# A fused attention and local-attention transformer kernel: K's projection around P's transposes, second parts of a norm's steps inside K's rotation, and the order of the first slots

## The chip, the cores and the metric

The kernel runs on one core of one Trainium2 chip. Its time is the device time of one execution in microseconds (us). A core has TensorE (PE, with its weight loads shown apart as PEld), VectorE (DVE), ScalarE (ACT), GpSimd (POOL) and SyncE (SP), which issues most DMAs. Each engine works through its own queue in order and waits for the others by semaphores.

## The reference

The input x has 4 batches of 512 tokens of width 128. First comes a pre-norm full attention with 16 heads of 64:

```python
x = x + attn(layernorm(x), Wq, Wk, Wv, Wr)
x = x + ffn_stack(layernorm(x), Wqkv, q_scale, k_scale, Wo, ln_g, ln_b, W1, b1, W2, b2)
```

The second line holds six layers, each of them

```python
x = attn_layer(shift_tokens(x), ...) + x
x = ffn_layer(shift_tokens(x), ...) + x
```

where shift_tokens moves half of the features by one token. attn_layer projects to q, k and v (3 x 1024 features), normalises each head of q and k by its length, scales and rotates them by position, and attends within windows of 32 tokens and the window before. ffn_layer is a layer norm with gain and bias, a projection to 2 x 341 features, a product of one half with the GELU of the other, and a projection back to 128. Everything is in 32-bit floats.

## The kernel before

The first attention takes the first 568 us of the trace and isn't touched. The layers work on *units* of 128 tokens: 6 layers x 4 batches x 4 tiles = 96 units, in the order layer, batch, tile. `slot(n, ...)` writes the instructions of one step of a software pipeline, by hand, and every engine then runs its own part in this order. In slot n four units are at work: `u` = unit n has its scores, exponentials and P times V; `prev` = n-1 its output projection and residual; `nxt` = n+1 its transposes of Q and K; `new` = n+2 its projections and rotations. The order in a slot is, by engine:

- TensorE: scores of u (L652, L663), Q's projection of new (L517), norm matmuls if any (L97, L106 or L114), output projection of prev (L720), the two groups of P's transposes (L625), K's projection, first half of P times V (L695), Q's transposes of nxt, V's projection, second half of P times V, K's transposes, an FFN chunk or the FFN's output if any (L763, L764, L783), and the transposes of the attention's output o.
- VectorE: maximum and subtraction for u (L673, L675), norm steps, the residual of prev (L728), Q's rotation (L538, L542), sum of Q's squares (L533), division of the first half of the attention's output (L704, L705), K's rotation, division of the second half, sum of K's squares, the start of the inverse norms (L557, L81, L82), and the FFN's gate (L771) or its residual (L786).
- POOL: for a first tile the shifted copies (L150 to L152) and, for a new layer, the rotation tables (L164, which waits for a small DMA); the rest of a norm's rsqrt (L84 to L87, 12 small operations), the two sums that end the rotations of Q and K (L553), the copy of K's last window (L644), 12 operations of the inverse norms, and the two multiplications by them (L561).
- ACT: the exponential (L681), the squares of Q and K (L528), all copies out of PSUM (L607, L628), GELU (L767), the square in a norm's mean step (L101).
- SP: the DMAs that lay out V in windows (L615 to L619), and the weights of the next layer behind the last unit of a layer.

PSUM holds three pairs of banks, called two0 to two2, which turn by one with each slot, and two single banks (`one_t`, in turn) for all transposes, the output projection and the norm's matmuls. So P's second group of transposes takes the bank that the output projection of the same slot was in, and waits for the residual to read it.

The FFN of a batch works beside the slots that follow its last unit. With n a multiple of 4, `plan` sets the shift at slot n, the three steps of its norm (mean, var, scale) at slots n+1, n+2 and n+3, between Q's projection and the output projection, the three chunks at n+3, n+4 and n+5 and the output at n+6, ahead of o's transposes. So a slot whose number leaves 1, 2 or 3 when divided by 4 has a norm step, and the others have the shifts. The first FFN chunk comes in slot 7. The norm of the last batch of the first attention, called `late`, runs ahead of slots 1, 2 and 3.

A layer norm's steps are: mean (a matmul with 1/128, the difference on VectorE, L99, and its square on ACT), var (small matmuls, L106, then the start of an rsqrt on VectorE, L81 and L82, and the rest on POOL), scale (transposes that spread the factor, L114, then the product, L118, and the gain and bias, L120).

Of the kernel before, what the change touches and what calls it, by code (L numbers as in the profile page):

```python
# [8 lines left out]
F32 = mybir.dt.float32  # L9
# [6 lines left out]
P = 128  # L16
# [16 lines left out]
def body(ctx: ExitStack, tc: tile.TileContext, a, out: bass.AP):  # L33
# [52 lines left out]
            eng.tensor_scalar(t, t, -0.5, 1.5, ALU.mult, ALU.add)  # L86
            eng.tensor_tensor(y if k < 2 else v, y, t, ALU.mult)  # L87

    def layernorm_steps(state, bank, inT, outT, g=None, b=None, eng=nc.vector, nt=NT, temp=tmpt):

        w = nt * P

        def mean():
            m = bank()[:, 0:w]
            mm(m, lhsT=avg, rhs=inT(), start=True, stop=True)  # L97
            xc = state["xc"] = temp()[:, 0:w]
            nc.vector.tensor_tensor(xc, inT(), m, ALU.subtract)  # L99
            sq = state["sq"] = temp()[:, 0:w]  # L100
            nc.scalar.activation(sq, xc, AF.Square)  # L101

        def var():
            v = bank()
            for t in range(nt):
                mm(v[:, t : t + 1], lhsT=state["sq"][:, t * P : (t + 1) * P], rhs=avg[:, 0:1], start=True, stop=True)  # L106
            rs = state["rs"] = small.tile([P, NT], F32, tag="rs", name="rs")[:, 0:nt]
            nc.vector.tensor_scalar(rs, v[:, 0:nt], EPS, None, ALU.add)  # L108
            rsqrt(rs, nt, eng)

        def scale():
            bc = bank()[:, 0:w]
            for t in range(nt):
                nc.tensor.transpose(  # L114
                    bc[:, t * P : (t + 1) * P], state["rs"][:, t : t + 1].to_broadcast([P, P]), ident
                )
            h = state["h"] = outT()
            nc.vector.tensor_tensor(h, state["xc"], bc, ALU.mult)  # L118
            if g is not None:
                nc.vector.tensor_scalar(h, h, g, b, ALU.mult, ALU.add)  # L120

        return mean, var, scale

# [48 lines left out]
    with tc.manual_schedule():  # L172
# [105 lines left out]
        class Rows:  # L278


            def __init__(self, b, c, t):
                self.b, self.c, self.t = b, c, t
# [212 lines left out]
    def two_t(k, name):  # L495
        k = (part[0] + k) % 3
        return ps.tile([P, 2, 512], F32, tag=f"two{k}", name=name, bufs=1)
# [7 lines left out]
    def flat(pt):  # L505
        return pt.rearrange("p a n -> p (a n)")
# [4 lines left out]
            self.i, self.b, self.T = i, b, T  # L511
            self.r = [None, None]

    def project(u, j):
        p = two_t((1, 2, 1)[j], "ps_proj")
        for c in range(2):
            mm(  # L517
                p[:, c, :],
                lhsT=u.xs[:, u.T * P : (u.T + 1) * P],
                rhs=wpart[j][:, c * 512 : (c + 1) * 512],  # L520
                start=True,
                stop=True,
            )
        return flat(p)

    def square(u, j):
        u.sq = s2a.tile([P, INNER], F32, tag="t1", name="sq", bufs=3)
# [4 lines left out]
            u.ss = small.tile([P, 2 * HEADS], F32, tag="ss", name="ss")  # L532
        nc.vector.tensor_reduce(u.ss[:, j * HEADS : (j + 1) * HEADS], heads(u.sq), AX.X, ALU.add)  # L533

    def rotate(u, j):
        t0 = u.r[j] = s2a.tile([P, INNER], F32, tag="rot", name="rot", bufs=6)
        lt, pf, half = u.lt, u.p[j], HD // 2
        nc.vector.tensor_tensor(  # L538
            heads(t0), heads(pf), lt[:, u.T, 2 * j].unsqueeze(1).to_broadcast([P, HEADS, HD]), ALU.mult
        )  # L540
        t1 = u.t1 = s2a.tile([P, INNER], F32, tag="t1", name="t1", bufs=3)
        nc.vector.tensor_tensor(  # L542
            t1.rearrange("p (h t d) -> p h t d", t=2, d=half),
            pf.rearrange("p (h t d) -> p h t d", t=2, d=half)[:, :, ::-1, :],
            lt[:, u.T, 2 * j + 1]
            .rearrange("p (t d) -> p t d", t=2)
            .unsqueeze(1)
            .to_broadcast([P, HEADS, 2, half]),
            ALU.mult,
        )  # L550
# [129 lines left out]
        u.prf = u.pr.rearrange("p c a n -> p (c a n)")  # L680
        nc.scalar.activation(u.prf, u.prf, AF.Exp)  # L681

    def transpose_p(u):
        u.pT = s2.tile([P, NC, P], F32, tag="pT", name="pT", bufs=2)
        for g in range(2):
            transposed(u.prf, g, u.pT, 0)

    def times_v(u, g, k=0):
        if g == 0:
# [41 lines left out]


    class Ffn:
        def __init__(self, u, t0=0, nt=NT, temp=tmpt, pair=None, eng=None):
            self.i, self.b, self.u, self.t0, self.nt, self.us, self.st = u.i, u.b, u, t0, nt, [], {}
            self.temp, self.pair = temp, pair or (lambda f: (tmpt(), tmpt()))
            self.mean, self.var, self.scale = layernorm_steps(
                self.st,
                one_t,
                lambda: self.xs,  # L740
                lambda: s2.tile([P, S], F32, tag="hT", name="hT", bufs=2)[:, 0 : nt * P],
                vecs[:, u.i, 0:1],
                vecs[:, u.i, 1:2],
                eng or nc.vector,
                nt,
                temp,
            )

        def shift(self):
# [81 lines left out]
        for v in units[u.n : u.n + NT]:  # L831
            v.xs, v.lt, v.p = xs, lt, [None] * 3

    def do_project(u, j):
        u.p[j] = project(u, j)
        if u.b + 1 == B and u.T + 1 == NT and u.i + 1 < L:
            wpart[j] = load_part(u.i + 1, j)

    def first_slot():
# [23 lines left out]
    def slot(n, norm, move, geglu):  # L863

        u, prev, nxt, new = unit(n), unit(n - 1), unit(n + 1), unit(n + 2)
        part[0] = n % 3
        begin(unit(n + 4))  # L870
        if u:
            scores(u)
            exponents(u)
        if new:
            do_project(new, 0)
            square(new, 0)
        if n == -1:
            y = one_t()
            project_out1(B - 1, y)
        for f in norm:  # L880
            f()
        if prev:
            project_out_2(prev)
            if prev.b + 1 == B and prev.T + 1 == NT and prev.i + 1 < L:
                wo_w[0] = load_wo(prev.i + 1)
            residual(prev)
        for f in move:
            f()
        if u:
            transpose_p(u)  # L890
        if new:
            rotate(new, 0)
            add_rotated(new, 0)
            sum_squares(new, 0)
        if n == -1:
            residual1(B - 1, y)
        if new:
            do_project(new, 1)
            square(new, 1)
        if u:  # L900
            times_v(u, 0)
        if nxt:
            transpose_q(nxt)
        if new:
            do_project(new, 2)
            v_windows(new, follower(new))
            rotate(new, 1)
            add_rotated(new, 1)
        if u:
            times_v(u, 1)  # L910
        if new:
            sum_squares(new, 1)
        if nxt:
            transpose_k(nxt)
        if n == -1:
            third_step()
        if nxt:
            carry_k(nxt, follower(nxt))
        if new:
            inverse_norms(new)  # L920
            over_norm(new, 0)
            over_norm(new, 1)
        for f in geglu:
            f()
        if u:
            transpose_o(u)

    with tc.manual_schedule():
        begin(units[0])
        late = norm_x1(one_t, B - 1)  # L930


        norm, move, geglu = {}, {}, {}

        def plan(steps, n, *fs):
            steps.setdefault(n, []).extend(fs)
# [3 lines left out]

        end = len(units)
        for n in range(NT, end - NT, NT):
            f = Ffn(units[n - 1], eng=nc.gpsimd)
            plan(move, n, f.shift)
            for k, g in enumerate((f.mean, f.var, f.scale)):
                plan(norm, n + 1 + k, g)
            for k in range(3):
                plan(geglu, n + 3 + k, at(f.chunk, k, 2))
            plan(geglu, n + 6, at(f.out, 2, n + 6 == end - 2))
        third, seq = f, Ffn(units[end - NT - 1], eng=nc.gpsimd)  # L950
        plan(move, end - 4, seq.shift)
        plan(norm, end - 3, seq.mean)
# [24 lines left out]
        def tail():  # L977

            exponents(u)
            seq.scale()  # L980
            project_out_2(prev)
            residual(prev)
            most.shift()
            transpose_p(u)
            most.mean()
            part[0] = 1
            times_v(u, 0, 0)
            times_v(u, 1, 1)
            part[0] = 0
            gate = seq.chunk(0, 0, True)  # L990
            transpose_o(u)
            gate()
            most.var()
            project_out_2(u)
            residual(u)
            last.shift()
            seq.chunk(1, 1)
            last.mean()
            most.scale()
            last.var()  # L1000
            seq.chunk(2, 2)
            for k in range(2):
                most.chunk(k, k)
            last.scale()
            most.chunk(2, 2)
            seq.out(0, True)
            for k in range(3):
                last.chunk(k, (k + 1) % 3)
            seq.finish()
            most.out(1, True)  # L1010
            last.out(2, True)
            most.finish()
            last.finish()

        first_slot()
        for n in range(-1, end - 1):
            if 1 <= n < 4:
                late[n - 1]()
            slot(n, norm.get(n, ()), move.get(n, ()), geglu.get(n, ()))
        tail()  # L1020

# [92 lines left out]
```

## Time and profile before

| | |
|---|---|
| median of 3 runs | 2260.88 us (2259.3 to 2263.07) |
| the profiled execution | 2261.35 us |
| its span on the core | 2259.6 us |
| first scores of slot 0 | 568.5 us |
| slots 37, 38, 39, 40, from scores to scores | 17.13, 18.37, 17.03, 16.54 us |
| slots 0 to 7 | 18.06, 16.89, 16.39, 15.14, 16.85, 15.96, 17.57, 17.30 us |
| granted clock of TensorE, mean | 0.993 |

A row of the timeline has the start and the length in us, the engine, the line of the code, the operation and its tiles, and in brackets the idle time just before it with what ended it. A row of the view of waits has the engine and line that waited, what it waited for, and the total in us, the number of waits and the longest one. A row of the view of windows has, for one stretch, its length, the busy time of PE, PEld, DVE, ACT and POOL (with the number of instructions), the granted clock of TensorE, the share of the DMA engines' time and GB/s.

### The profile page before, as it was taken

The page shows a single profiled execution, that of the slowest core. Times are in us where ns is not written, and L with a number is a line of the kernel's source. Part 1 is how long each engine was busy: PE and PEld are TensorE (multiplying, and loading weights), DVE is VectorE, ACT ScalarE, POOL GpSimd, SP SyncE. Part 2 cuts the span into 40 slices and gives each one's busy share as a digit, 9 for nine tenths or more (in the row PEclk, how much of TensorE's full clock was granted, in tenths as well). Part 3 has the DMA queues.
Part 4 walks back from the last instruction along what each step waited for, and adds up shares of the span by engine and source line. Part 5 has one row for each costly group of instructions (what it writes and reads, how often), then busy time and mean ns, then how long its engine had stood idle before and what let it go on. Part 6 is the DMA issues. An engine that isn't in the chain of part 4 may idle for free.

```text
span 2259.6 us, 82472 instructions
## 1 busy us (share of the span) xinstructions
PE 2183.4 (97%) x35150; PEld 1435.4 (64%) x35150; DVE 1710.3 (76%) x2501; ACT 1365.9 (60%) x2589; POOL 1511.7 (67%) x2281
## 2 busy tenths in 40 slices
PE   7999999999899999999999999999999999999997
PEld 5565655554666666666666666666666666666665
DVE  4676667676778888878788788878888788888874
ACT  4665656564556656666566656666566666666663
POOL 2554545465787777777777777777777777777762
PEclk8999999999999999999999999999999999999999
DMA  3000000000322233232322323223232223322221
GB/s 117 1 1 1 1 1 1 1 1 9 75 69 60 69 87 73 57 76 69 85 69 62 78 66 86 66 67 73 71 85 63 66 71 87 76 63 70 60 67 28
DMA packets 91064, 125.77 MB, mean 56 GB/s; under 512 B 25422, under 2 KB 39500, under 8 KB 90700
## 3 DMA queue, kind: packets, MB, share of 16 engines
q1 hardware_dynamic: 89996, 118.79, 21.4%
q8 instruction: 280, 4.59, 0.9%
q10 hardware_dynamic: 704, 1.70, 0.2%
q14 instruction: 84, 0.69, 0.1%
HBM read 20.31 MB, written 1.05 MB: 9 GB/s over the span
## 4 chain that ended last, share of the span: by engine, by line
PE 58%; DVE 12%; POOL 3%; issue 2%; ACT 1%; POOLq 0%; ACTq 0%
PE ps_proj L517 18%; PE ps_one L625 14%; PE ps_att L663 6%; PE ps_att L695 6%; PE ps_one L720 3%; PE ps_proj L783 3%; PE ps_proj L763 3%; PE ps_proj L764 3%; DVE y L82 2%; DVE mx L673 2%; DVE pr L675 2%; PE ps_att L652 1%; DVE hT L120 1%; POOL rot L553 1%; DVE t L542 1%
## 5 line engine op out<-in xcount | busy, mean ns | idle before, releaser
L553 POOL TENSOR_TENSOR rot<-rot,t 128x1024 f32<-128x1024 f32 x192 | 453.9, 2365 | 255.8 <-DVE t L542 188.5
L517 PE MATMUL ps_proj<-wqkv,xs 128*128 128x512 f32 x1152 | 557.0, 606 | 5.9 <-DVE tmp_t L771 5.0
L344 POOL TENSOR_TENSOR pr<-pr,den 128x1024 f32<-128x1024 f32 x128 | 241.0, 1894 | 247.5 <-DVE den L341 239.6
L561 POOL TENSOR_TENSOR rot<-rot,ss 128x1024 f32<-128x1024 f32 x192 | 361.5, 1904 | 7.4
L517 PEld LDWEIGHTS ps_proj<-wqkv,xs 128*128 128x128 f32 x1152 | 197.5, 191 | 157.2 <-issue 143.2
L528 ACT ACTIVATE sq<-ps_proj 128x1024 f32<-128x1024 f32 x192 | 195.3, 1017 | 127.5 <-PE ps_proj L517 126.8
L681 ACT ACTIVATE pr<-pr 128x1024 f32<-128x1024 f32 x96 | 101.5, 1058 | 260.8 <-DVE pr L675 260.8
L542 DVE TENSOR_TENSOR t<-ps_proj,lt 128x1024 f32<-128x1024 f32 x192 | 233.2, 1215 | 19.6 <-POOL rot L553 19.2
L538 DVE TENSOR_TENSOR rot<-ps_proj,lt 128x1024 f32<-128x1024 f32 x192 | 233.0, 1214 | 19.5 <-ACT sq L528 19.4
L533 DVE TENSOR_REDUCE ss<-sq 128x16 f32<-128x1024 f32 x192 | 231.6, 1206 | 0.0
L330 ACT ACTIVATE pr<-ps_sc,nm 128x128 f32<-128x128 f32 (+3 forms) x448 | 220.6, 511 | 5.7 <-DVE nm L317 5.2
L317 DVE TENSOR_REDUCE nm<-ps_sc 128x2 f32<-128x1024 f32 x128 | 155.9, 1218 | 82.8 <-PE ps_sc L305 82.7
L673 DVE TENSOR_REDUCE mx<-ps_att 128x16 f32<-128x1024 f32 x96 | 117.5, 1224 | 127.1 <-PE ps_att L663 127.1
L625 PE MATMUL ps_one<-ident,rot 128*128 128x128 f32 x1536 | 209.6, 279 | 0.9 <-POOL rot L561 0.9
L720 PEld LDWEIGHTS ps_one<-aT,wo 128*128 128x128 f32 x1536 | 183.0, 192 | 24.6 <-issue 23.9
L720 PE MATMUL ps_one<-aT,wo 128*128 128x128 f32 x1536 | 189.1, 276 | 0.4 <-DVE rs L108 0.3
L625 PEld LDWEIGHTS ps_one<-ident,rot 128*128 128x128 f32 x1536 | 164.7, 141 | 19.8 <-POOL rot L561 1.1
L695 PEld LDWEIGHTS ps_att<-vw,pT 64*32 64x32 f32 x9216 | 101.1, 105 | 108.3 <-issue 108.0
L607 ACT COPY vt<-ps_proj 128x512 f32<-128x512 f32 x192 | 103.2, 590 | 101.3 <-PE ps_proj L517 101.3
L355 PEld LDWEIGHTS ps_pt<-ident,pr 128*128 128x128 f32 x1024 | 118.2, 142 | 56.9 <-issue 47.1
L84 POOL TENSOR_TENSOR yt<-y 128x32 f32<-128x32 f32 (+2 forms) x384 | 88.0, 229 | 93.6 <-DVE y L82 47.5
L355 PE MATMUL ps_pt<-ident,pr 128*128 128x128 f32 x1024 | 135.7, 275 | 3.0 <-POOL pr L344 2.7
(173 smaller groups left out, 4083.0 us busy)
## 6 DMA issues: line engine op xcount, KB each, us to landing
vw<-vt SPq DMA_DIRECT2D x1152, 65.0 KB, 2.0
vw_first<-vt SPq DMA_DIRECT2D x336, 65.0 KB, 2.0
wqkv<-in_wqkv_dram SPq DMA_DIRECT2D x18, 512.0 KB, 9.2
wo<-in_wo_dram SPq DMA_DIRECT2D x6, 512.0 KB
w<-in_w_dram SPq DMA_DIRECT2D x6, 341.0 KB, 3.5
xr<-in_x_dram SPq DMA_DIRECT2D x3, 256.0 KB
scales<-in_scales_dram SPq DMA_DIRECT2D x6, 128.0 KB, 3.2
w<-in_w_dram SPq DMA_DIRECT2D x12, 64.0 KB, 2.9
```

The source lines that it names most:

```text
L330: nc.scalar.activation(self.pr[:, h, cols], self.sc[:, h, cols], AF.Exp, bias=self.nm[:, part_, h : h + 1], accum_out=self.den[:, part_, h ...
L344: nc.gpsimd.tensor_tensor(self.pr, self.pr, self.den[:, 0].unsqueeze(2).to_broadcast([P, 2, S]), ALU.mult)
L355: nc.tensor.transpose(pt[:, k * P : (k + 1) * P], self.pr[:, h, k * P : (k + 1) * P], ident)
L517: mm(p[:, c, :], lhsT=u.xs[:, u.T * P : (u.T + 1) * P], rhs=wpart[j][:, c * 512 : (c + 1) * 512], start=True, stop=True,)
L533: nc.vector.tensor_reduce(u.ss[:, j * HEADS : (j + 1) * HEADS], heads(u.sq), AX.X, ALU.add)
L538: nc.vector.tensor_tensor(heads(t0), heads(pf), lt[:, u.T, 2 * j].unsqueeze(1).to_broadcast([P, HEADS, HD]), ALU.mult)
L542: nc.vector.tensor_tensor(t1.rearrange("p (h t d) -> p h t d", t=2, d=half), pf.rearrange("p (h t d) -> p h t d", t=2, d=half)[:, :, ::-1, :],
L553: nc.gpsimd.tensor_tensor(u.r[j], u.r[j], u.t1, ALU.add)
L561: nc.gpsimd.tensor_tensor(heads(u.r[j]), heads(u.r[j]), u.ss[:, j * HEADS : (j + 1) * HEADS].unsqueeze(2).to_broadcast([P, HEADS, HD]), AL ...
L625: nc.tensor.transpose(tp[:, c * P : (c + 1) * P], src[:, (4 * g + c) * P : (4 * g + c + 1) * P], ident)
L695: mm(o[j * W : (j + 1) * W, h, c * (HD + 1) : (c + 1) * (HD + 1)], lhsT=u.pT[h * HD : (h + 1) * HD, 4 * g + c, j * W : (j + 1) * W], rhs=u ...
L720: mm(y[:, 0:P], lhsT=wo_w[0][:, c, :], rhs=u.aT[:, c, :], start=(c == 0), stop=(c == NC - 1))
```

## The change

It has five parts.

1. K's projection is made in two halves of 512 columns. In a slot with a norm step the first half stands between the two groups of P's transposes, in another slot ahead of both; the second half follows the second group. Slot 0 has the whole projection ahead of P's transposes, and Q's transposes of nxt ahead of the first half of P times V.
2. The norm steps of the FFNs in the loop put their second part on a list, `later`: the square in mean, the rsqrt in var, gain and bias in scale. K's rotation runs that list between its two operations on VectorE.
3. In slots without an FFN part (up to slot 6) K's rotation and its sum on POOL come behind the second half of P times V instead of ahead of it.
4. The three steps of `late` run as norm steps of slots 0, 1 and 2.
5. In the last layer the transposes and the output DMA that finish a batch (`finish`) come one slot after the FFN's output (slot 91 instead of 90).

```diff
+        def then(f):
+            f() if later is None else later.append(f)
...
-            nc.scalar.activation(sq, xc, AF.Square)
+            then(lambda: nc.scalar.activation(sq, xc, AF.Square))
...
-            rsqrt(rs, nt, eng)
+            then(lambda: rsqrt(rs, nt, eng))
...
-                nc.vector.tensor_scalar(h, h, g, b, ALU.mult, ALU.add)
+                then(lambda: nc.vector.tensor_scalar(h, h, g, b, ALU.mult, ALU.add))
...
-    def project(u, j):
-        p = two_t((1, 2, 1)[j], "ps_proj")
-        for c in range(2):
+    def project(u, j, c0=0, c1=2):
+        p = u.p[j] if c0 else two_t((1, 2, 1)[j], "ps_proj")
+        u.p[j] = p
+        for c in range(c0, c1):
...
-    def rotate(u, j):
+    def rotate(u, j, between=()):
...
+        for f in between:
+            f()
...
-    def transpose_p(u):
-        u.pT = s2.tile([P, NC, P], F32, tag="pT", name="pT", bufs=2)
-        for g in range(2):
-            transposed(u.prf, g, u.pT, 0)
+    def transpose_p(u, g):
+        if g == 0:
+            u.pT = s2.tile([P, NC, P], F32, tag="pT", name="pT", bufs=2)
+        transposed(u.prf, g, u.pT, 0)
...
+        if n == 0:
+            do_project(new, 1)
         if u:
-            transpose_p(u)
+            if norm:
+                transpose_p(u, 0)
+        if new and n != 0:
+            do_project(new, 1, 0, 1)
+        if u:
+            if not norm:
+                transpose_p(u, 0)
+            transpose_p(u, 1)
         if new:
             rotate(new, 0)
             add_rotated(new, 0)
...
         if new:
-            do_project(new, 1)
+            if n != 0:
+                do_project(new, 1, 1)
             square(new, 1)
+        if nxt and n == 0:
+            transpose_q(nxt)
         if u:
             times_v(u, 0)
-        if nxt:
+        if nxt and n != 0:
             transpose_q(nxt)
         if new:
             do_project(new, 2)
             v_windows(new, follower(new))
-            rotate(new, 1)
-            add_rotated(new, 1)
+            if geglu:
+                rotate(new, 1, later)
+                add_rotated(new, 1)
         if u:
             times_v(u, 1)
         if new:
+            if not geglu:
+                rotate(new, 1, later)
+                add_rotated(new, 1)
+            later.clear()
             sum_squares(new, 1)
...
-        norm, move, geglu = {}, {}, {}
+        norm, move, geglu = {k: [f] for k, f in enumerate(late)}, {}, {}
...
-            f = Ffn(units[n - 1], eng=nc.gpsimd)
+            f = Ffn(units[n - 1], eng=nc.gpsimd, later=later)
...
-            plan(geglu, n + 6, at(f.out, 2, n + 6 == end - 2))
+            ends = f.i + 1 == L
+            plan(geglu, n + 6, at(f.out, 2, ends))
+            if ends and n + 6 < end - 2:
+                plan(geglu, n + 7, f.finish)
...
-            if 1 <= n < 4:
-                late[n - 1]()
             slot(n, norm.get(n, ()), move.get(n, ()), geglu.get(n, ()))
```

## The prediction

> **What bounds the kernel now.** First the page's busy times and chain, for which engine sets the end.
>
> ```profile
> span 2259.6 us, 82472 instructions
> PE 2183.4 (97%) x35150; PEld 1435.4 (64%) x35150; DVE 1710.3 (76%) x2501; ACT 1365.9 (60%) x2589; POOL 1511.7 (67%) x2281
> PE 58%; DVE 12%; POOL 3%; issue 2%; ACT 1%; POOLq 0%; ACTq 0%
> ```
>
> TensorE does. DVE's 12% of the chain is the time in which TensorE hangs on VectorE, and the view of waits says where in the layers:
>
> ```profile
> PEld ps_one L625 <- DVE xT L728: 32.6, 69, 1.7
> PEld ps_one L625 <- ACT pr L681: 8.5, 27, 3.0
> ```
>
> L625 is the helper for all transposes; the form that waits is P's. Its second group takes the PSUM bank that the output projection's y was in, so it waits until the residual (L728) has read y. The first group waits for the exponential (L681). Next the timeline of a settled stretch, slots 38 and 39 (18.37 and 17.03 us, start of scores to start of scores; 37 and 40 take 17.13 and 16.54), VectorE and POOL around L728:
>
> ```profile
> 1227.64 3.76 POOL L561 TENSOR_TENSOR rot<-rot,ss 128x1024 f32<-128x1024 f32 x2
> 1229.60 1.83 DVE L82 TENSOR_SCALAR y<-yt 128x4 int32<-128x4 int32 x1
> 1231.34 0.28 DVE L728 TENSOR_TENSOR xT<-ps_one,xT 128x128 f32<-128x128 f32 x1
> 1241.12 0.18 DVE L82 TENSOR_SCALAR y<-yt 128x32 int32<-128x32 int32 x1
> ...
> 1245.26 3.77 POOL L561 TENSOR_TENSOR rot<-rot,ss 128x1024 f32<-128x1024 f32 x2
> 1248.09 1.22 DVE L120 TENSOR_SCALAR hT<-hT,vecs 128x512 f32<-128x512 f32 x1
> 1249.56 0.66 PE L625 MATMUL ps_one<-ident,pr 128*128 128x128 f32 x4 [0.25 <-DVE xT L728]
> ```
>
> L82 needs 0.18 us, but takes 1.83 and ends when POOL's pair of multiplications ends (1231.43 against 1231.40); L120 ends 0.28 after its pair (1249.31 against 1249.03), so 0.28 is its own price. Both stand ahead of L728. POOL's long operations hold VectorE's SBUF-to-SBUF tensor_scalar back, and through L728 they hold TensorE.
>
> **The change, part by part.** n mod 4 tells the slots apart: 1 has the FFN norm's mean, 2 its var, 3 its scale, 0 the shifts on POOL.
>
> (1) K's projection is split around P's second group: 0.9 us (2 of the L517 pieces of 1.88 per four) lie between the groups in slots with a norm, ahead of both in the others. It needs nothing late: its PSUM pair was read in the slot before. No instruction is added, and the split is free: in the starts of single matmuls the one after a change between a 128x512 and a transpose follows at the usual 0.43 or 0.11 us. L728 finishes about 0.35 us after the output projection and the second group now comes 1.35 after it. So the 32.6 us go, but for some 2 in the last two slots, which are not changed, and 1.5 in slots 1 to 7, counted below: -29. In the 22 slots with n mod 4 = 0 the wait for the exponential, 0.18 each on the weight load, is covered too: -4.
>
> (2) The second parts of the norm's steps go between K's two rotation operations. L81, L82 and L120 then run while POOL has finished the first rotation's sum (L553, 2.36 us) and waits for K's: 0.2 + 0.2, and 0.28. Here a rule is weighed. The Trainium skill, "SBUF — State Buffer", Who interferes with whom, says that a tensor_scalar in a two-port mode and a GpSimd instruction exclude each other for a whole instruction, whoever is first. The rows agree, and the rule also speaks against the change: it moves POOL's sums as well. In a var slot POOL's 12 small steps (3.3 us, 1231.5 to 1234.8) leave the place ahead of Q's sum for that ahead of K's, so K's sum starts about 2.5 us after its operands; L557, L81 or L82 then collide with it. By the free rows they cost 0.6, by the rule up to 2.4 more. I take the rule: L786, next on VectorE and the reader of the FFN's PSUM pair, then ends at 1243.9 on the trace's clock, and Q's next projection, which takes that pair, is due at 1243.9 with slot 38's gain taken off. The cover is used up: 0.05 x 22 = +1 (0 to 0.45 each). ACT's square of the mean slot (0.62) falls between V's copies and K's; Q's next projection has 0.5 us left: nothing.
>
> (3) What is late next. VectorE's string from L728 to the end of L82 was 9.7 us in slot 39 and gets L120's 0.28 and a longer block at L557 (about +0.3), while TensorE gains 1.1 in slots 38 and 39. POOL's multiplications then end 7.9 us into slot 40, not 7.1; the two shifts (2.85) follow, Q's sum starts at 10.75, not 9.96, K's second rotation waits for it, and the gate (L771), which frees Q's PSUM pair, ends 18.2 us after the slot's start. Q's projection could begin at 18.0. I take 0.3 x 17 = +5 (0 to 0.8 each). In the other five (12, 28, 44, 60, 76) POOL has a layer's table to make as well, and the stall there already exists:
>
> ```profile
> 1345.79 2.28 DVE L81 TENSOR_SCALAR yt<-ss 128x32 int32<-128x32 int32 x1
> 1349.11 3.68 PE L517 MATMUL ps_proj<-wqkv,xs 128*128 128x512 f32 x4 [1.75 <-DVE tmp_t L771]
> 1349.00:1352.00 3.00, 2.89 (x4) 1.34 (x5) 2.41 (x3) 0.52 (x1) 2.19 (x10) 0.54 0.38 85
> ```
>
> POOL is 0.8 us later there: 5 x 0.8 = +4. The third line is a window's row; its clock, 0.54, is why the projection takes 3.68 and not 1.88. The skill's "TensorE: Matmul & The Clock Gate" (HAM clock gate) puts the half rate after an idle window of about 3.4 us; here a wait of 1.75 was enough, though 2.16 in slot 0 was not. By the page new stalls under 2 us cost only themselves, by this row perhaps 1.7 us on top. The row decides; it goes into the range.
>
> (4) Slots up to 6 have no FFN chunk, and there K's rotation moves behind the second half of P times V. The reason is in slot 4:
>
> ```profile
> 649.03 1.23 DVE L542 TENSOR_TENSOR t<-ps_proj,lt 128x1024 f32<-128x1024 f32 x1 [2.26 <-POOL rot L553]
> 651.24 0.63 PE L625 MATMUL ps_one<-ident,on 128*128 128x128 f32 x4 [1.60 <-DVE on L705]
> 569.38 1.32 DVE L557 TENSOR_SCALAR ss<-ss 128x32 f32<-128x32 f32 x1
> ```
>
> That stall and its like in slots 0 and 2 (1.27 and 0.6) vanish. But from the end of P times V VectorE now has, in a row, the division (0.95), two rotations (2.3), the squares' sum (1.2), L557 blocked by K's sum as in the third line (1.3), L81 and L82 (0.5), maximum and subtraction (2.5): then the exponential (1.1). With latencies P's first group comes 9.9 us after P times V, and the next one ends 7.05 (6.15 in slots 3 and 4) later: 16.9 or 16.0 us a slot, where slots 1 to 6 took 16.89, 16.39, 15.14, 16.85, 15.96 and 17.57. In slot 0 K's whole projection and the late norm's mean fill the 2.16 us wait for the exponential, about -1.9 by the first scores of slot 1. Carried through slot by slot, K's sum behind the var steps of slot 6 makes Q's transposes of slot 7 wait 1.8 us for POOL. Net at slot 8: +3 (-3 to +8).
>
> (5) The finish of batch 0 leaves slot 90 for 91, where its operands are old:
>
> ```profile
> 2150.32 0.63 PE L801 MATMUL ps_one<-ident,xT 128*128 128x128 f32 x4 [1.66 <-DVE xT L788]
> ```
>
> 1.66, the slower transposes after it and part of a half-clock window: -3.
>
> Sum: -29 - 4 + 1 + 5 + 4 + 3 - 3 = -23. Against the profiled span 2259.6 that is 2236.6; the median of the runs lies 1.3 above the span: 2238.
>
> **The rivals.**
> A, everything hides: nothing is late in (2) and (3), the start is even: -29 - 4 - 3 + 1, so 2226. For it: VectorE is busy 13.9 of a mean 17.3 us a slot, POOL 12.9. Against it: both run in strings with waits, and the cover of 0.9 us in n mod 4 = 0 is all used by my count.
> B, POOL takes over: the shifts' slots stall 0.8 each (14), the table slots 1.5 (7), the var slots 0.2 (4), the start costs 5: 33 + 3 less 30 leaves 6, so 2255. For it: POOL's operations don't shrink while TensorE's slots do. Against: in slot 40 L771 starts at 1276.59, as ACT's Gelu ends (1276.56), so it had some time to lose before POOL decides.
> C, slower: in the shifts' slots L557 is caught by Q's sum and L81 by K's, back to back, as in slots 44 and 60 (1.75 and 2.28 us). That stall with its half clock costs about 3.9 us. It decides from 9 of 22 slots (33 + 3 - 3 = 33 us); at 12 the time is 2275. Against: without the table Q's sum ends some 3 us before L557 is issued.
> D, gains and losses cancel within 0.2% (4.5 us, what a measurement of this kernel can tell from no change): the change doesn't do what it says, as the waits reappear at Q's projection.
>
> **How the numbers follow.** Forecast 0.48 (2230 to 2246), A 0.20, B 0.20, C 0.07, D 0.05. The range 2224 to 2257 takes in A and most of B and leaves out C and the far ends. Faster: 0.48 + 0.20 + 0.17 of B = 0.85; same 0.05 + 0.02 of B = 0.07; slower 0.08.
>
> **What would show it.** Right: L625 waits no more for L728 outside the end; L82 of 128x4 and L120 at about 0.2 and 0.3 us in the mean (they are 1345 and 1294 ns); slots of 17.0, 17.8, 16.6 and 16.5 us; no wait at L801 in the middle. Wrong: waits of L517 for L771 at each fourth slot (B, C), L557 over 1 us as a rule, slots 1 to 7 above 17 us, or a clock below 1 in more windows than now.

## The result, and the profile after

The changed kernel takes 2249.19 us (median; 2241.36 to 2259.39), the kernel before 2261.03 (2253.23 to 2264.26): a ratio of 0.9952, with an interval of 0.9939 to 0.9965. The forecast was 2238. So the change gains 11.8 us where 23 were expected; 2249 lies in the range that the prediction gave, 11 us above its forecast and 6 below rival B (2255). The profiled execution has a span of 2249.4 us.

The first rows of the page after (span, busy times, the chain by engine):

```profile
span 2249.4 us, 82469 instructions
PE 2171.9 (97%) x35150; PEld 1435.0 (64%) x35150; DVE 1701.7 (76%) x2501; ACT 1366.3 (61%) x2589; POOL 1512.9 (67%) x2281
PE 50%; DVE 13%; POOL 9%; issue 3%; ACT 1%; ACTq 0%; POOLq 0%
```

TensorE's share of the chain fell from 58 to 50%; VectorE's stayed (12 to 13%), and POOL's rose from 3 to 9%: the chain now runs more through POOL, and not more through TensorE. Next the view of waits, TensorE's matmuls (PE) and weight loads (PEld), three rows of before and then five of after; the transposes' helper is now L632 (L625 before), the residual L735 (728), the FFN chunk's first line L771 (763), the second half of K's rotation L549 (542), Q's projection L521 (517), the FFN's gate L779 (771):

```profile
PE ps_one L625 <- DVE xT L728: 17.5, 44, 1.4
PE ps_proj L763 <- DVE t L542: 1.6, 3, 0.8
PE ps_proj L517 <- DVE tmp_t L771: 5.0, 4, 2.5
```

```profile
PEld ps_one L632 <- ACT pr L688: 10.9, 15, 2.1
PEld ps_one L632 <- DVE xT L735: 1.4, 2, 1.2
PEld ps_proj L771 <- DVE t L549: 19.6, 19, 1.3
PE ps_proj L771 <- DVE t L549: 15.1, 19, 1.0
PE ps_proj L521 <- DVE tmp_t L779: 8.0, 4, 2.8
```

P's second group waited 32.6 us for the residual, counted on the weight loads; 1.4 are left, in the last two slots. In their place the FFN chunk waits for K's second rotation, up to 1.0 us, 19 times: in each of the 16 shift slots without a table, and in slots 7, 13 and 61. Before, that pair had three such waits, 1.6 us in all. Q's projection waits for the gate four times, as before, and never behind a shift slot without a table. (The waits for the exponential, the first row of after, are now mostly those of slots 2 to 5; step 4 below comes back to them.)

The timeline of slots 38 and 39, rows of VectorE, POOL and TensorE, against the one shown of before:

```profile
1227.67 3.77 POOL L568 TENSOR_TENSOR rot<-rot,ss 128x1024 f32<-128x1024 f32 x2
1230.88 0.29 DVE L735 TENSOR_TENSOR xT<-ps_one,xT 128x128 f32<-128x128 f32 x1 [1.73 <-PE ps_one L727]
1231.98 0.60 PE L632 MATMUL ps_one<-ident,pr 128*128 128x128 f32 x4
1236.64 0.17 DVE L82 TENSOR_SCALAR y<-yt 128x4 int32<-128x4 int32 x1
1240.15 2.35 POOL L560 TENSOR_TENSOR rot<-rot,t 128x1024 f32<-128x1024 f32 x1
1240.15 2.39 DVE L81 TENSOR_SCALAR yt<-ss 128x32 int32<-128x32 int32 x1
1248.30 0.29 DVE L735 TENSOR_TENSOR xT<-ps_one,xT 128x128 f32<-128x128 f32 x1 [0.96 <-PE ps_one L727]
1254.14 0.54 DVE L123 TENSOR_SCALAR hT<-hT,vecs 128x512 f32<-128x512 f32 x1
```

The residual now runs while POOL's pair is still going (1227.67 to 1231.44), and P's second group starts 0.8 us after it without a wait. L82 takes 0.17 (1.83 before) and the last multiplication of the scale, L123, 0.54 (1.22). In the var slot the block has moved to L81, which starts with K's sum on POOL and ends 0.04 after it. Slots 38 and 39 take 17.9 and 16.6 us (18.4 and 17.0).

Then slot 40, one of the *shift slots*, those with n mod 4 = 0. Five of these (12, 28, 44, 60 and 76) also make a new layer's table on POOL and are called *table slots* here. First before, then after (its scores begin at 1259.81 and at 1258.73); POOL's sum for Q, K's second rotation, the chunk:

```profile
1269.77 2.36 POOL L553 TENSOR_TENSOR rot<-rot,t 128x1024 f32<-128x1024 f32 x1
1272.16 1.22 DVE L542 TENSOR_TENSOR t<-ps_proj,lt 128x1024 f32<-128x1024 f32 x1
1273.66 1.02 PE L763 MATMUL ps_proj<-hT,w 128*128 128x512 f32 x2
```

```profile
1262.87 3.76 POOL L568 TENSOR_TENSOR rot<-rot,ss 128x1024 f32<-128x1024 f32 x2
1268.82 0.61 POOL L155 COPY tmp_t<-xT 64x511 f32<-64x511 f32 x1
1269.52 2.37 POOL L560 TENSOR_TENSOR rot<-rot,t 128x1024 f32<-128x1024 f32 x1
1271.92 1.23 DVE L549 TENSOR_TENSOR t<-ps_proj,lt 128x1024 f32<-128x1024 f32 x1 [1.04 <-POOL rot L560]
1273.20 1.12 PE L771 MATMUL ps_proj<-hT,w 128*128 128x512 f32 x2 [0.70 <-DVE t L549]
```

Before, the rotation ended at 1273.38 and the chunk, which takes the PSUM pair that the rotation reads, began at 1273.66: no wait, and 0.28 us to spare. After, Q's sum starts 10.79 us into the slot and not 9.96, and most of the 0.83 us arrives at the chunk: it starts 14.47 us into the slot and not 13.85, its first pair of matmuls takes 1.12 and not 1.02, and the slot takes 17.26 us and not 16.54.

Slot 40 is one of the milder cases. Over the 16 shift slots without a table (medians), Q's sum starts at 10.85 and not 9.88, the chunk at 14.53 and not 13.66, and it follows the rotation's end by 0.05 to 0.06 us in every slot of after, where it was 0.16 before (from 0.05 to 0.52).

Why K's second rotation should wait for Q's sum at all needs a word, since it uses nothing that this sum makes. It is the buffer. The squares and the results of the second rotations share three buffers in SBUF (tag t1 in the code). In the program as built, K's second rotation of slot 40 is written into the buffer with the result of Q's, which Q's sum must read first. So it is for 90 of the 96 units, in the kernel before and in the changed one; the exceptions are the five table slots and one early unit.

The slots are timed from start of scores to start of scores in the two profiled executions; summed by kind they give the whole difference:

| stretch (us) | before | after | change | forecast |
|---|---|---|---|---|
| start of slot 0 | 568.5 | 567.8 | -0.7 | 0 |
| slots 0 to 7 | 134.1 | 138.3 | +4.2 | +3 |
| n mod 4 = 1, 2, 3, from slot 8 on, without slot 90 and those behind a table slot | 1020.6 | 993.8 | -26.8 | -29 + 1 |
| 16 shift slots without a table, and slot 92 | 278.9 | 292.7 | +13.8 | +5 - 3 |
| 5 table slots, each with the next | 179.4 | 179.9 | +0.5 | +4 - 1 |
| slot 90 | 21.6 | 17.8 | -3.8 | -3 |
| slots 94 and 95 with the end | 56.5 | 59.2 | +2.7 | 0 |
| sum | 2259.6 | 2249.4 | -10.2 | -23 |

(The -4 of the exponential in slots with n mod 4 = 0 is put here as -3 in the ordinary and -1 in the table slots.) One row carries the miss: the shift slots. The last row is a stretch at half clock that this execution has in its tail and that of before has not, as a window of the profile after shows (its clock is the 0.52):

```profile
2221.00:2228.00 7.00, 6.75 (x25) 5.35 (x25) 0.83 (x5) 0.81 (x3) 2.34 (x12) 0.52 0.01 2
```

### The profile page after: what moved, and what is told of

It reads as the page before. It is cut to its first block, busy times and chain, and to the rows that moved or that the text cites. A ratio compares the mean times of both kernels' runs of the same rounds, so it can differ in the third digit from the quotient of the medians.

```text
span 2249.4 us, 82469 instructions
## 1 busy us (share of the span) xinstructions
PE 2171.9 (97%) x35150; PEld 1435.0 (64%) x35150; DVE 1701.7 (76%) x2501; ACT 1366.3 (61%) x2589; POOL 1512.9 (67%) x2281
## 3 DMA queue, kind: packets, MB, share of 16 engines
q1 hardware_dynamic: 89996, 118.79, 21.6%
## 4 chain that ended last, share of the span: by engine, by line
PE 50%; DVE 13%; POOL 9%; issue 3%; ACT 1%; ACTq 0%; POOLq 0%
PE ps_proj L521 14%; PE ps_one L632 10%; PE ps_one L727 5%; PE ps_att L670 5%; PE ps_att L702 4%; DVE t L549 3%; POOL rot L560 3%; PE ps_proj L791 3%; POOL rot L568 3%; PE ps_proj L771 2%; PE ps_proj L772 2%; DVE ss L538 2%; DVE rot L543 2%; DVE pr L682 1%; DVE mx L680 1%
## 5 line engine op out<-in xcount | busy, mean ns | idle before, releaser
L521 PE MATMUL ps_proj<-wqkv,xs 128*128 128x512 f32 x1152 | 569.9, 604 | 9.0 <-DVE tmp_t L779 8.0
L521 PEld LDWEIGHTS ps_proj<-wqkv,xs 128*128 128x128 f32 x1152 | 189.6, 191 | 115.4 <-issue 97.1
L549 DVE TENSOR_TENSOR t<-ps_proj,lt 128x1024 f32<-128x1024 f32 x192 | 233.5, 1216 | 26.2 <-POOL rot L560 26.2
L632 PE MATMUL ps_one<-ident,rot 128*128 128x128 f32 x1536 | 209.6, 279 | 3.1 <-POOL rot L568 2.0
L632 PEld LDWEIGHTS ps_one<-ident,rot 128*128 128x128 f32 x1536 | 164.7, 141 | 22.1 <-POOL rot L568 3.7
L635 ACT COPY pT<-ps_one 128x512 f32<-128x512 f32 x192 | 110.0, 586 | 87.6 <-PE ps_one L632 87.1
```

What stands on the lines that cost most here:

```text
L521: mm(p[:, c, :], lhsT=u.xs[:, u.T * P : (u.T + 1) * P], rhs=wpart[j][:, c * 512 : (c + 1) * 512], start=True, stop=True,)
L549: nc.vector.tensor_tensor(t1.rearrange("p (h t d) -> p h t d", t=2, d=half), pf.rearrange("p (h t d) -> p h t d", t=2, d=half)[:, :, ::-1, :],
L632: nc.tensor.transpose(tp[:, c * P : (c + 1) * P], src[:, (4 * g + c) * P : (4 * g + c + 1) * P], ident)
```

## The experiments

The theory from this table: the change saves what was forecast in the slots with a norm step, but POOL's shifts come ahead of Q's sum in the shift slots, so Q's sum is late, K's second rotation behind it, and the chunk behind that. The rivals: the splitting of the norm's steps itself makes POOL late; VectorE's own string is the bound; the wait sits at Q's next projection, as forecast (the rows of waits above already speak against it: 5.0 and 8.0 us, four waits each). The last two columns are slot sums of the profiled execution as above: the 16 shift slots without a table (without slot 92), and the slots with n mod 4 = 1 to 3.

| kernel | median us (range) | ratio to before (interval) | shift slots | mod 1 to 3 |
|---|---|---|---|---|
| before | 2261.03 | 1 | 262.6 | 1020.6 |
| the change | 2249.19 | 0.9952 (0.9939 to 0.9965) | 276.6 | 993.8 |
| e1, FFN's shift behind Q's sum | 2246.26 (2245.02 to 2249.91) | 0.9944 (0.9924 to 0.9964) | 259.5 | 994.6 |
| e2, both shifts and the table late | 2225.65 (2224.79 to 2227.55) | 0.9851 (0.9832 to 0.9870) | 259.5 | 994.3 |
| e3, without the second parts | 2253.08 (2251.47 to 2255.96) | 0.9966 (0.9953 to 0.9979) | 274.5 | 1003.1 |
| e4, without the split | 2259.09 (2250.26 to 2265.75) | 0.9991 (0.9980 to 1.0002) | 274.2 | 1002.7 |
| e5, rotation first in every slot | 2243.27 (2241.63 to 2246.70) | 0.9930 (0.9909 to 0.9950) | 276.5 | 996.0 |
| e6, e2 and e5 together | 2214.66 (2213.52 to 2216.76) | 0.9793 (0.9779 to 0.9808) | 258.9 | 994.6 |
| e7, e2 without the split | 2238.52 (2237.76 to 2240.48) | 0.9899 (0.9884 to 0.9914) | 262.4 | 1004.5 |
| e8, FFN's shift twice | 2293.57 (2290.39 to 2296.18) | 1.0150 (1.0130 to 1.0171) | 319.2 | 994.4 |
| e9, before with both shifts and the table late | 2247.98 (2244.92 to 2250.23) | 0.9938 (0.9922 to 0.9955) | 261.7 | 1021.4 |

**e1, one shift out of the way.**

```diff
-        for f in move:
-            f()
...
             rotate(new, 0)
             add_rotated(new, 0)
+        for f in move:
+            f()
+        if new:
             sum_squares(new, 0)
```

> The changed kernel, with the FFN's shift (two POOL copies, 1.4 us) moved from ahead of Q's sum to behind it in the slots whose number is a multiple of 4. Theory POOL: in these slots Q's sum is late, K's second rotation waits for it, and the FFN's chunk, which takes K's PSUM pair, waits for that rotation (15.1 us on TensorE in 19 waits). Then 1.4 us less ahead of the sum takes the waits to under 3 us in all, these slots go from 17.3 to about 16.4 us, and the time is about 2234 us; K's sum loses nothing, since POOL idles 1.4 us ahead of it. Theory ORDER: what costs the time there is the new place of K's first half ahead of both groups of P's transposes, or gain and bias in VectorE's string; POOL then changes nothing: 17.3 us and 2249 us.

The ordinary shift slots fell from 17.3 to 16.2 us, and the chunk's wait left them: the lateness is POOL's, and taking the FFN's shift, 1.3 us, from ahead of Q's sum is enough to end it. But the time, for which 2234 was expected, fell by only 3, no more than the two intervals leave open, because the five table slots rose, with the next ones, from 179.9 to 194.2. The timeline of e1 in slot 44, POOL's table and Q's sum, then VectorE's K rotation and the chunk:

```profile
1333.81 2.37 POOL L167 TENSOR_TENSOR lt<-tabs,scales 128x1024 f32<-128x1024 f32 x1 [1.57 <-DVE on L712]
1336.13 2.36 POOL L560 TENSOR_TENSOR rot<-rot,t 128x1024 f32<-128x1024 f32 x1
1338.52 1.23 DVE L549 TENSOR_TENSOR t<-ps_proj,lt 128x1024 f32<-128x1024 f32 x1 [3.71 <-POOL rot L560]
1339.80 1.12 PE L771 MATMUL ps_proj<-hT,w 128*128 128x512 f32 x2 [3.18 <-DVE t L549]
```

In the changed kernel K's rotation of this slot waits for nothing (1338.84, with Q's sum only at 1341.98): in the table slots it is written into the buffer of Q's squares. In e1 it is written there into the buffer of Q's second rotation, as in the other slots, and waits for the sum, which is behind the table. The wait at the chunk is the same chain, three times as long.

**e2, everything of POOL's that isn't urgent behind the sums.** e1's edit, and the next units' shift and the layer's table behind K's sum; the load of the scales stays where it was.

```diff
-        begin(unit(n + 4))
+        rest = begin(unit(n + 4))
...
             sum_squares(new, 1)
+        rest()
         if nxt:
             transpose_k(nxt)
```

> As the run with the FFN's shift behind Q's sum, and also the next units' shifted copies and a new layer's table behind K's sum (the DMA of the scales stays where it was). Theory POOL: the slots after a new layer's table (13, 29, 45, 61, 77, which take 18.65, 21.32, 21.06, 18.35 and 19.28 us) go to about 17 us as well, some 14 us more, about 2220 us, and no clock window at half rate there. Theory ORDER: 2249 us; a table that is moved only moves its wait, to Q's transposes of the next slot.

2225.65 us, 23.5 under the changed kernel. Slot 40 of e2 begins at 1251.65 (same rows; its lines stand 5 higher):

```profile
1261.37 2.36 POOL L565 TENSOR_TENSOR rot<-rot,t 128x1024 f32<-128x1024 f32 x1 [1.73 <-DVE t L554]
1264.24 1.22 DVE L554 TENSOR_TENSOR t<-ps_proj,lt 128x1024 f32<-128x1024 f32 x1
1265.77 1.02 PE L776 MATMUL ps_proj<-hT,w 128*128 128x512 f32 x2
```

Q's sum starts 9.7 us into the slot (9.06 in the median of the 16), after a wait of POOL for VectorE and not the other way round. K's second rotation still goes to the buffer of Q's, but the sum that it must wait for is over in time. The chunk waits for nothing. Ordinary shift slots take 16.2 us, table slots with the next 169.5 together (179.9). The chain by engine has gone back to TensorE:

```profile
PE 64%; DVE 5%; POOL 4%; issue 2%; ACT 1%; POOLq 0%; ACTq 0%
```

**e3 and e4, one half of the change at a time.**

```diff
 e3
-            f = Ffn(units[n - 1], eng=nc.gpsimd, later=later)
+            f = Ffn(units[n - 1], eng=nc.gpsimd)
 e4
-        if u:
-            if norm:
-                transpose_p(u, 0)
-        if new and n != 0:
-            do_project(new, 1, 0, 1)
-        if u:
-            if not norm:
-                transpose_p(u, 0)
-            transpose_p(u, 1)
+        if u:
+            transpose_p(u, 0)
+            transpose_p(u, 1)
+        if new and n != 0:
+            do_project(new, 1, 0, 1)
```

> The changed kernel with the norm's steps whole again (the square, the rsqrt and the last multiplication stay in the step, ahead of the residual), K's projection still split. Theory (the split gives 0.9 us of cover to the residual; second parts matter little): L82 and L120 are blocked again by POOL's pair of multiplications, the residual is up to 1.3 us later, but K's half projection and the bank's 0.35 us hide most of it; slots with n mod 4 = 2 and 3 are 0 to 0.3 us longer than in the changed kernel, shift slots (n mod 4 = 0) stay at 17.0 to 17.3 us, since POOL's shifts still stand ahead of Q's sum. Time 2247 to 2260. Rival (the second parts made POOL late, through K's sum): the shift slots fall to 16.4 us and the time to 2238. Other rival (the second parts were the larger half of the gain): P's second group waits for the residual 13 us or more as in the run without the split, and the time is 2258 or above.

> The changed kernel without the split: both groups of P's transposes stand ahead of K's projection again (slot 0 keeps its own order); the second parts of the norm's steps stay inside K's rotation. If the second parts are what held the residual, the second group waits only some 0.1 us as in mean slots of the kernel before: slots 1, 2, 3 mod 4 take about 17.1, 17.9, 16.7 us, the shift slots 17.2, and the time is about 2253 us. If the split is what matters, 0.4 to 0.6 us come back in slots 2 and 3: about 2262 us.

Either half alone shortens the slots with a norm's step by about 18 us (1020.6 to 1003.1 and 1002.7), both together by 27: they partly save the same waits. And either half alone lengthens the 16 shift slots, by 11.9 and 11.6 us. So the lateness is not due to the split alone, nor to the second parts alone. What the two have in common is that TensorE gains time in the slots ahead while POOL's work stays as long; that this is the reason is argued from here, not tested by itself. The waits for the residual, and for the chunk, in e3 and then in e4:

```profile
PEld ps_one L632 <- DVE xT L735: 31.3, 43, 1.3
PE ps_one L632 <- DVE xT L735: 3.5, 9, 0.9
PE ps_proj L771 <- DVE t L549: 12.9, 19, 1.0
```

```profile
PEld ps_one L632 <- DVE xT L735: 13.4, 68, 1.0
PE ps_proj L771 <- DVE t L549: 9.9, 19, 1.0
```

In e3 the residual is late as before, and weight loads wait for it as long as ever, 31.3 us; but they now wait beside the half projection, and the matmuls wait 3.5 where they waited 17.5. In e4 the wait is 13.4 us in 68 waits, about 0.2 each: with the small steps out of its way the residual is no longer held back by POOL. By time e4 can't be told from the kernel before.

**e7 and e9, the same with the shifts late.** e7 is e2 with e4's edit, e9 the kernel before with nothing but e2's two moves.

> The changed kernel without the split of K's projection, but with the shifts and the table behind the sums. Theory (two separate matters: the split saves P's waits for the residual and for the exponential, the shifts' place sets the wait of the FFN chunk): shift slots 16.3 to 16.4 us (16.19 with the split), the other slots as in the run without the split, 17.14, 18.07 and 16.66; so 0.15 x 65 + 0.2 x 21 = 14 us more than with the split: 2240. Rival (both are one lateness of POOL, and the cure of one cures the other): within 4 us of 2225.7. Other rival (the split is needed for the late shifts to pay): 2250 or above.

> The kernel before, with nothing but its shifts and table moved behind the sums, as in the run that did this to the changed kernel. Theory (in the kernel before the shift slots had no wait for POOL: 16.34 us; only the five table slots had one): the shift slots stay at 16.2 to 16.4, P's second group still waits some 30 us for the residual, the table slots and the next ones fall from 16.3 and 18.2 to 21.5 to about 16.2 and 17.6, some 10 us with their half-clock windows: 2250. Rival (late shifts are worth the same 23 us in any order of the rest): 2238.

Both came within some 2 us of the theory (2240 and 2250). With the shifts out of the way the change is worth 2248.0 - 2225.65 = 22.3 us, 9.5 of them without the split (e9 to e7) and 12.9 by it (e7 to e2); with the shifts in place it was worth 11.8. In the kernel before, late shifts bring nothing in the ordinary shift slots (262.6 to 261.7); its 13 us come from the table slots (179.4 to 169.5) and from slots 0 to 7 (134.1 to 131.1). P's waits stay:

```profile
PEld ps_one L630 <- DVE xT L733: 34.7, 69, 1.7
```

**e8, the suspected cost doubled.**

```diff
             if c0 == 0:
                 shift_into(xs, src[:, 0:n], n)
+                shift_into(xs, src[:, 0:n], n)
```

> The changed kernel with the FFN's shift made twice into the same buffer (three more POOL instructions of 0.10, 0.61 and 0.61 us ahead of Q's sum in each shift slot; the first writing is left without a reader). Theory (the chunk L771 takes K's PSUM pair, so it waits for K's second rotation, this for Q's sum, this for the shifts): POOL's 1.3 us arrive whole, L771's waits go from 1.0 to 2.3 us in the 17 ordinary shift slots, and these from 17.3 to 18.6 us: +22 us, and up to 1.7 us more in each slot in which the clock is halved after such a wait: 2271, up to 2300. In the slots with a layer's table less. Rival (the shift slots are long because of VectorE's own string, or because Q's next projection waits for the gate): the slots grow by less than half of the added time, 2259 or less.

2293.6 us. The chunk (L772 here) waits 39.1 us in place of 15.1. Two shift slots of e8, 40 and 48, by the chunk's row, and a window's row behind the first (its clock is the 0.64):

```profile
PE ps_proj L772 <- DVE t L549: 39.1, 21, 2.5
1288.17 2.07 PE L772 MATMUL ps_proj<-hT,w 128*128 128x512 f32 x2 [1.87 <-DVE t L549]
1429.33 1.13 PE L772 MATMUL ps_proj<-hT,w 128*128 128x512 f32 x2 [2.21 <-DVE t L549]
1287.00:1291.80 4.80, 3.63 (x6) 1.50 (x7) 4.06 (x7) 1.31 (x2) 3.13 (x4) 0.64 0.47 108
```

Slot 48 took 18.56 us, 1.24 over the changed kernel's: POOL's 1.3 us arrive nearly whole. Slot 40 took 20.42, because the clock was halved for 3.4 us behind the wait. 3 of the 16 ordinary shift slots are of the first kind (18.55 to 18.56) and 13 of the second (20.0 to 20.4, median 20.26, so 1.7 us for the clock). The slots with n mod 4 = 1 to 3 did not change.

**e5 and e6, the first slots.** e5 puts K's rotation ahead of the second half of P times V in all slots, and not only in those with an FFN chunk.

```diff
-            if geglu:
-                rotate(new, 1, later)
-                add_rotated(new, 1)
+            rotate(new, 1, later)
+            add_rotated(new, 1)
         if u:
             times_v(u, 1)
         if new:
-            if not geglu:
-                rotate(new, 1, later)
-                add_rotated(new, 1)
             later.clear()
```

> The changed kernel with K's rotation ahead of the second half of P times V in the first slots too. Theory of the prediction: behind it, VectorE has all its work in one string from P times V to the maximum, and POOL's sum blocks L564 for 1.4 us in it, so slots 1 to 7 took 132.7 us against 117.1. With the rotation first these slots go back to some 126 us: the first scores of slot 8 at about 700 instead of 706.1 us, the time about 2244 us. Rival: the rotation in front brings back the waits of the attention output's transposes for the division, 1.3 to 1.6 us in slots 2 and 4, and the early slots gain nothing: 2249 us.

> The changed kernel with both moves that helped by themselves: the shifts and the layer's table behind the sums (2225.65 us alone), and K's rotation ahead of the second half of P times V in the first slots too (5.9 us less alone: 2243.3 against 2249.2). They act in different slots, so they should add: 2219.7 us (2217 to 2223), first scores of slot 8 some 6 us sooner, shift slots 16.2 us, table slots 16 to 17.9. Rival (they share a wait, because the first slots' shifts also stand ahead of the rotations there): half or less of the 5.9 remains, 2223 or above.

(In its expectation two sums are wrong: by the traces slots 1 to 7 took 122.7 us after and 116.1 before.) e5 brings slots 0 to 7 from 138.3 to 132.1 us and the time from 2249.2 to 2243.3; the shift slots stay as they were (276.5): that part of the change costs 6 us. With it and e2's moves (e6) they take 129.2, and the time is 2214.66, 2.1% under the kernel before. The two gains add, and more, so that the time lies below the 2217 to 2223 expected: e6 is 11.0 under e2, of which 9.1 lie in slots 0 to 7. Why they are more than e5's 6.2 was not followed up (slot 2 takes 18.7 us in e2, 17.4 in the changed kernel).

## Why the prediction was right and wrong

**Step (1), the waits of P: right.** The 32.6 us of waits are 1.4, and slots with n mod 4 = 1 to 3 lost 26.8 us (forecast -28 with step (2)'s +1). The exponential's 0.18 each shows in e7 against e2, without the split and with it: 16.34 and 16.19 us in the shift slots. e3 shows why the split works, cover and not an earlier residual.

**Step (2), the rule weighed: right, with one size off.** L81 is blocked for 2.39 us by K's sum in the var slot, as the rule of the Trainium skill, "SBUF — State Buffer" (Who interferes with whom), has it: 2.1 more than the 0.30 that it takes in slot 40, and the free rows would have missed it. Slot 39 shows no wait for it. The last multiplication was misread: 0.28 us was what was left of it when POOL's pair ended, and its own price is 0.54.

**Step (3), what is late next: this failed.** Its first half was right: in slot 40 POOL's multiplications end 7.9 us in, as forecast, and Q's sum starts 10.79 in, where 10.75 was forecast (10.85 in the median of the shift slots). Its second half took the wrong deadline. "and the gate (L771), which frees Q's PSUM pair, ends 18.2 us after the slot's start. Q's projection could begin at 18.0. I take 0.3 x 17 = +5" looks two instructions too far down. The gate does end 18.17 us in, but by then Q's projection has been pushed back to 19.02 and has nothing to wait for:

```profile
1276.15 0.74 DVE L779 SCALAR_TENSOR_TENSOR tmp_t<-ps_proj,vecs,tmp_t 128x512 f32<-128x512 f32 x1
1277.75 1.98 PE L521 MATMUL ps_proj<-wqkv,xs 128*128 128x512 f32 x4
```

What pushed it back is the chunk, which takes the pair that K's rotation still reads. The kernel before had little to spare there, 0.28 us in slot 40 and 0.16 in the median, in rows that could have been read (L542's end at 1273.38, L763's start at 1273.66). In the 16 shift slots the chunk's weight loads now wait 16.6 us for the rotation, 1.04 each (12.8 us by the starts of the matmuls, 0.80 each; the ends of the matmuls before them are modelled). Less the exponential's 0.16, that is the 0.88 by which these slots grew, 14.0 us in all. So the term of +5 should have been some +17 before the exponential's gain, or +14 after it, and the sum -11: 2250, where 2249 was measured. The prediction's own upper end, "0 to 0.8 each", and rival B's 14 us for these slots were near this size; B's reason, that POOL takes over, was the right one here. That the chain is this one is shown by e1, e2 and e8: with the shift behind the sum the wait goes, with the shift made twice it grows by about as much.

The table slots were put at +4 and gave +0.5 with their next; their waits were there before, and a part of them is set by which buffer K's rotation has (e1). Why they lost less than forecast was not followed up. C did not come: in slot 44 the two blocks stand back to back (L564 2.33 us, L81 2.27), in slot 40, without a table, the same lines take 0.55 and 0.30.

**Step (4), the first slots: right in size, and in part by luck.** +4.2 in slots 0 to 7, +3.5 at the first scores of slot 8, forecast +3. Slot by slot it was less near, and the misses partly cancel: the first scores of slot 1 came 3.1 us sooner where 1.9 was forecast, and slot 5 took 18.1 us where 16.9 was. In slots 2 to 5 P's first group now waits 1.8 to 2.1 us each for the exponential (weight loads), the price of VectorE's longer string; in e5, with the rotation first, none of slots 1 to 6 waits for it over 0.24. Of its pieces, the squares' scale is blocked by K's sum (1.37 us, forecast 1.3), Q's transposes of slot 7 wait 1.46 for POOL (forecast 1.8), and the chunk of slot 7 waits as well, which was not foreseen:

```profile
653.66 1.37 DVE L564 TENSOR_SCALAR ss<-ss 128x32 f32<-128x32 f32 x1
697.65 1.09 PE L632 MATMUL ps_one<-ident,rot 128*128 128x128 f32 x8 [1.46 <-POOL rot L568]
703.28 1.13 PE L771 MATMUL ps_proj<-hT,w 128*128 128x512 f32 x2 [1.00 <-DVE t L549]
```

**Step (5), the finish: right.** Slot 90 lost 3.8 us (forecast 3), and the wait of 1.66 at the finish's transposes is gone from the view of waits. No run has this part alone, but slot 90 stays at 21.6 us in e9, which lacks it, and takes 17.7 to 18.2 in all runs that have it.

So in the profiled execution the sum missed by 13 us: 12 in the shift slots, 2.7 in the tail's clock, and 2.5 back in the table slots, with about 1 us in the rest.

## What to carry to other kernels

When TensorE gains in some slots of a round, the strings on the other engines keep their length, so they come late, relative to it, in the next slot: find the first instruction there that takes what they release, and read how much it has to spare, before a later and more visible deadline is worked out. Look also at which buffer that instruction's releaser writes to: here a rotation waited for a sum that it does not need, because both used one buffer. Here 0.2 to 0.3 us of spare, where a string came 0.8 to 1.0 later, turned a gain of 27 us into one of 13, and it was won back by moving two shifts and a table, which nobody was waiting for just then, behind the sums that the chain was waiting for. A fourth buffer, so that K's rotation needn't wait for Q's sum, was not tried. A change that shows half its worth may be whole: measured on top of that move it gave 22 us.

## What the runs showed of the hardware

The halved clock does not follow from the length of a wait alone. In e8 a wait of 1.87 us was followed by 3.4 us at half clock, one of 2.21 was not, as the two rows above show. In each run the starts of such stretches stand whole multiples of 3.413 us apart (in e8, 14 of them from 721.6 to 2145.0 us, to within 0.01 us). Laid on that grid, TensorE's idle time in one 3.413 us window tells them apart: over the eleven profiles, from 600 us to 8 us before the last matmul, each window at full clock with over 1.81 us idle was followed by half clock, none with under 1.57 was, and those between went both ways (32 stretches in all; the ends of matmuls are modelled). Two windows of e1 that were themselves at half clock had 1.96 and 2.99 us idle, and full clock followed. In the three shift slots of e8 that were spared, the wait lay across a border of the grid. The Trainium skill, "TensorE: Matmul & The Clock Gate" (HAM clock gate), has the free-running window of about 3.4 us, and that agrees; it asks for an idle window, and here about half a window was enough. So the chunk's waits of 0.6 to 1.0 us cost themselves alone here, and one of 2 us costs 1.7 more where it falls within one window, which in e8 was 13 times in 16. Where the grid lies is, as far as these runs show, chance: the same tail has such a stretch in the profiles of after, e1, e2 and e4 and none in those of the other seven kernels.
